# Two group norms share two borders of an attention on one Trainium2 core, and one image's statistics change their place

## The chip, the cores and the metric

The kernel runs on 1 core of one Trainium2 chip, as one program. The metric is the device time of one execution in microseconds (us). It is compared by medians of several runs. The engines of the core that matter here are TensorE (PE: matrix products, with weight loads, PEld, that overlap them), VectorE (DVE), ScalarE (ACT), GpSimd (POOL) and SyncE (SP), which issues most of the DMA transfers.

## The reference

Eight images of 512 channels and 32 x 32 pixels go through two attention blocks. Layer 0 has 8 heads of 64 channels, and its group norm has 32 groups; layer 1 has one head of 512 channels, and its group norm has 8 groups. All numbers are f32.

```python
# layer 0
h = group_norm(x, gn_weight, gn_bias)                  # GROUPS = 32
qkv = jnp.einsum('oc,bct->bot', w_qkv, h.reshape(B, C, T)) + b_qkv[None, :, None]
weight = softmax(jnp.einsum('bct,bcs->bts', q * scale, k * scale))
a = jnp.einsum('bts,bcs->bct', weight, v)
x = x + (jnp.einsum('oc,bct->bot', w_proj, a) + b_proj[None, :, None])
# layer 1
xn = group_norm(x, gamma, beta)                        # GROUPS = 8
q, k, v = conv1x1(xn, ...)
attn = softmax(jnp.einsum('bqc,bck->bqk', q, k) * scale)
x = x + conv1x1(jnp.einsum('bqk,bkc->bqc', attn, v), p_w, p_b)
```

A group norm takes the mean and the variance over the channels of a group and all pixels, and then scales and shifts each channel.

## The kernel before, in words

**Tiling.** An image is four tiles of 128 channels x 1024 pixels. The 1x1 convolutions are Strassen-like products of seven terms, nested twice (`conv2`, `inner_steps`), so that VectorE and GpSimd add blocks while TensorE multiplies. The results of TensorE lie in PSUM tiles; a tile of 128 partitions x 512 f32, which is what `acc_tile` gives out, fills one bank. `acc_tile` has two buffers.

**Order of work.** The main loop of `main_path` runs over the images b. Each pass runs `attention0` of image b, then layer 1 of image b - 1 (`layer1_scores`, `layer1_rest`), then the value, key and query convolutions of image b + 1 (`values`, `keys_and_queries`), then the projection of image b (`projection2`). The first pass has no layer 1, and the last one is laid out otherwise. Every product on TensorE goes through the helper `matmul` at L60, which keeps it in the order of the program text; so a product that waits holds back all later ones. On the other engines a planner places instructions by their traced order and its own forecast of when they are ready, unless one is pinned by `keep_in_program_order`.

**Hooks.** Small work is handed to the large stages as lists of functions. A `conv2` takes four lists, one for each outer pair of its products, called after the pair's seventh step. `attention0` takes the list `extra`: for each of its eight rounds (four pairs of heads by two halves of the pixels) one entry after the round's scores `sc` and one after its products `av`. In a round TensorE makes eight blocks of scores (tiles of 64 rows x 128 columns of the array), ScalarE turns each into `e` (L696), VectorE adds them up in `sum` (L698, L700), and TensorE then multiplies `e` by the values into `av` (tiles of 128 x 64). Entries 4 and 5 are the two borders of the third round: between its scores and its products, and between its products and the next round's scores.

**The norms.** `GroupNorm` computes a norm in four steps. `stats` runs two `bn_stats` and one `bn_aggr` for a channel tile on VectorE (L91, L96). `group_mean` (L107 on) multiplies the means by the matrix of groups on TensorE, copies the product out of PSUM (L113) and makes `dv` of it in three further VectorE instructions (L115, L117, L119). `affine` (L121 on) multiplies `dv` by the same matrix, adds the epsilon on VectorE (`ve`, L124) and makes the scale and the shift in four GpSimd instructions (L126 to L132). `apply` uses them on ScalarE. With `halves` a product is made as two products of 64 columns, the form that the `av` products have; without it as one of 128 columns. Each f32 product appears as two matmul instructions in the trace.

Layer 1's norm of image b, made in `projection2`, puts its two products into entries 4 and 5 of `attention0` of image b + 1. Layer 0's norm of image b + 2 is made in `values` during the pass of image b; its statistics run in the background of the value convolution (in the first pass they are pinned in the value convolution's last two hooks), and its two products stand in the first and third hook of the key convolution, in `keys_and_queries`. There are six such norms of layer 0, for images 2 to 7; the pass of image 6 has none. The norm of image 0 and that of image 1 are made in the prologue. What `affine` yields for image b + 2 is first used in `layer1_rest` of the next pass, where the image is loaded again and normed.

## Time and profile before

| what | value |
|---|---|
| time, median of 3 runs (lowest to highest) | 2768.54 us (2767.63 to 2768.78) |
| time of the profiled execution | 2768.3 us |
| its span, from the first instruction to the last | 2765.8 us |
| granted clock of TensorE, mean | 0.999 |
| products of `gmean` and of `gvar` on TensorE, instructions each | 46 (28 of 128 x 64, 18 of 128 x 128) |
| `rstd` on GpSimd (L126), mean of 16 | 1177 ns |
| `d` (L115) on VectorE, median | 164 ns |
| VectorE busy in the key convolution of the first pass (258.7 to 280.3 us) | 16.56 of 21.60 us |
| VectorE busy in the value convolution of the first pass (233.5 to 258.7 us) | 18.68 of 25.20 us |

How to read it: the span runs from the program's first recorded instruction to its last, and the time of the same execution is 2.5 us longer. Busy time of an engine is the union of its instructions. A row of the timeline gives the start and the length in us, the engine, the line, the operation, what it writes and reads, the shape, how many instructions are merged, and in brackets how long the engine was idle before and what ended that.

### The profile page before, as it was taken

What the parts mean: (1) busy time and instruction counts of PE and PEld (TensorE: products, weight loads), DVE (VectorE), ACT (ScalarE), POOL (GpSimd) and SP (SyncE); (2) the same over time, 40 slices, a digit from 0 to 9 for tenths busy, and PEclk for the clock granted to TensorE, in tenths of its full rate; (3) what the DMA queues carried; (4) which work ended last, traced back from release to release, by engine and by line L of the source; (5) the groups of instructions that cost most, each with busy time, mean ns of one, the idle gap of its engine ahead of it and who ended that gap; (6) DMA issues with size and microseconds to landing.
All of it is one profiled execution on the core that took longest, in us unless ns stands there. A gap on an engine that the chain in (4) does not pass through costs nothing.

```text
span 2765.8 us, 36809 instructions
## 1 busy us (share of the span) xinstructions
PE 2753.6 (100%) x13436; PEld 1762.1 (64%) x13436; DVE 2045.6 (74%) x3214; ACT 998.4 (36%) x1307; POOL 1291.4 (47%) x1384
## 2 busy tenths in 40 slices
PE   9999999999999999999999999999999999999999
PEld 5437736776376853868538694486844968348585
DVE  6587777777777777777777867777678776787776
ACT  1253454214632146312453125531255313633130
POOL 2313605745067440774307752176621766146763
PEclk9999999999999999999999999999999999999999
DMA  7827412344113441144401443114521145112302
GB/s 265 253 91 252 181 32 70 138 159 166 40 63 138 170 162 32 63 161 167 150 24 63 177 182 119 32 55 184 196 98 49 58 153 216 59 54 97 142 24 74
DMA packets 126070, 332.60 MB, mean 120 GB/s; under 512 B 19831, under 2 KB 64695, under 8 KB 114362
## 3 DMA queue, kind: packets, MB, share of 16 engines
q1 hardware_dynamic: 125294, 329.75, 33.6%
q8 instruction: 108, 1.77, 0.3%
q14 instruction: 80, 0.66, 0.1%
q10 hardware_dynamic: 588, 0.42, 0.1%
HBM read 258.14 MB, written 71.99 MB: 119 GB/s over the span
## 4 chain that ended last, share of the span: by engine, by line
PE 99%; DVE 1%; DMA 0%; issue 0%; SPq 0%; DVEq 0%
PE sc L60 16%; PE av L60 16%; PE psb_av L60 6%; PE psb L60 5%; PE psa_av L60 4%; PE psc_av L60 4%; PE psc L60 4%; PE psa L60 3%; PE psb_v L60 3%; PE psb_k L60 3%; PE psb_p L60 3%; PE psb_q L60 3%; PE psb_g L60 3%; PE psb_z L60 3%; PE psc_z L60 2%; PE psa_k L60 2%
## 5 line engine op out<-in xcount | busy, mean ns | idle before, releaser
L700 DVE TENSOR_TENSOR sum<-sum,e 128x1024 f32<-128x1024 f32 x384 | 473.9, 1234 | 35.5 <-ACT e L696 0.9
L696 ACT ACTIVATE e<-sc 128x1024 f32<-128x1024 f32 x512 | 476.1, 1053 | 63.1 <-PE sc L60 62.6
L60 PE MATMUL sc<-q,k 64*128 64x512 f32 x2048 | 456.8, 596 | 0.0
L60 PE MATMUL av<-e,v 128*64 128x512 f32 x2048 | 453.4, 595 | 0.0
L60 PEld LDWEIGHTS sc<-q,k 64*128 64x128 f32 x2048 | 190.1, 185 | 245.9 <-ACT e L696 120.9
L60 PEld LDWEIGHTS av<-e,v 128*64 128x64 f32 x2048 | 141.4, 137 | 299.0 <-issue 288.2
L434 POOL TENSOR_TENSOR inner_h<-x 128x256 f32<-128x256 f32 x16 | 14.8, 924 | 415.9 <-DVE x L1028 415.9
L698 DVE TENSOR_TENSOR sum<-e,e 128x1024 f32<-128x1024 f32 x64 | 79.9, 1249 | 103.6 <-ACT e L696 103.6
L719 ACT COPY a<-av 128x512 f32<-128x512 f32 x64 | 37.5, 586 | 320.1 <-PE av L60 280.6
L126 POOL TENSOR_TENSOR rstd<-ve,mhalf 128x4 f32<-128x4 f32 x16 | 18.8, 1177 | 274.0 <-DVE ve L124 274.0
L60 PE MATMUL psb<-inner,inner_h 128*128 128x256 f32 x448 | 115.6, 380 | 0.0
L60 PE MATMUL psa_av<-e,z 128*128 128x512 f32 x256 | 112.5, 592 | 0.0
L482 ACT COPY psb_v<-psa_v 128x512 f32<-128x512 f32 (+1 forms) x28 | 14.5, 517 | 232.5 <-DVE x L845 176.6
L60 PEld LDWEIGHTS psb<-inner,inner_h 128*128 128x128 f32 x448 | 84.5, 190 | 13.6 <-POOL inner L449 2.1
L60 PE MATMUL psb_z<-w_z,inner_h 128*128 128x128 f32 x672 | 87.5, 276 | 0.0
L60 PE MATMUL psb_g<-inner_h,w_m 128*128 128x256 f32 x336 | 84.9, 381 | 0.0
L776 ACT ACTIVATE e<-e 128x1024 f32<-128x1024 f32 x64 | 65.1, 1052 | 46.7 <-DVE e L766 25.6
L60 PEld LDWEIGHTS psb_z<-w_z,inner_h 128*128 128x128 f32 x672 | 81.4, 192 | 0.5
L60 PEld LDWEIGHTS psa_av<-e,z 128*128 128x128 f32 x256 | 47.4, 190 | 53.6 <-issue 51.7
L771 POOL TENSOR_TENSOR e<-e,e 128x512 f32<-128x512 f32 x64 | 79.3, 1271 | 2.0 <-DVE e L766 1.8
L571 POOL TENSOR_TENSOR v<-v,v 128x256 f32<-128x256 f32 x28 | 20.1, 726 | 125.3 <-DVE u_v L566 121.3
L820 POOL TENSOR_TENSOR t<-e,t 128x1024 f32<-128x1024 f32 x32 | 78.4, 2482 | 0.0
(443 smaller groups left out, 6138.0 us busy)
## 6 DMA issues: line engine op xcount, KB each, us to landing
r<-all_rows SPq DMA_DIRECT2D x78, 256.0 KB
x<-in_x SPq DMA_DIRECT2D x36, 512.0 KB
h<-in_x SPq DMA_DIRECT2D x32, 512.0 KB
spill<-x SPq DMA_DIRECT2D x32, 512.0 KB
x<-spill SPq DMA_DIRECT2D x32, 512.0 KB
out<-x SPq DMA_DIRECT2D x63, 256.0 KB
kept<-a SPq DMA_DIRECT2D x28, 512.0 KB
again<-kept SPq DMA_DIRECT2D x28, 512.0 KB
```

What stands on the lines that cost most here:

```text
L60: tc.keep_in_program_order(nc.tensor.matmul(*args, **kw))
L126: nc.gpsimd.tensor_tensor(rstd, ve, mhalf, ALU.pow)
L434: pin(engine.tensor_tensor(dst, x, y, ALU.subtract))
L482: nc.scalar.copy(ps["b"], ps["a"])
L571: nc.gpsimd.tensor_tensor(d, x, y, ALU.add)
L696: nc.scalar.activation(e, sc, AF.Exp, scale=(C // 8) ** -0.5)
L698: nc.vector.tensor_add(total, es[0], e)
L700: nc.vector.tensor_add(total, total, e)
L719: nc.scalar.copy(dst, av)
L771: nc.gpsimd.tensor_tensor(blocks(dst, r, cc)[0], blocks(x, r, cc)[0], blocks(y, r, cc)[0], ALU.add)
L776: nc.scalar.activation(e[c, cc, r], e[c, cc, r], AF.Exp, scale=scale)
L820: on = lambda *a: lambda: tc.keep_in_program_order(nc.gpsimd.tensor_tensor(*a))
```

## The change

Layer 0's norm of image b + 2 gets `halves=True` and is handed, as `ahead`, to `projection2`. Its two products leave the key convolution for entries 4 and 5 of the next pass's attention. There each entry allocates one PSUM tile and calls the two norms one after the other: layer 1's norm on columns 0 to 3, then layer 0's on columns 4 to 7, with `start=False`. In the first pass the third image's statistics leave the value convolution's hooks 2 and 3 and stand, one channel tile at a time and still pinned, in the four hooks of the key convolution.

```diff
-        def over_group(self, ps, rhs):
+        def over_group(self, ps, rhs, start=True):
             for cols in (ts(0, 64), ts(1, 64)) if self.halves else (slice(0, P),):
-                matmul(ps[cols, :], gm[:, self.layer, cols], rhs, start=True, stop=True)
+                matmul(ps[cols, :], gm[:, self.layer, cols], rhs, start=start, stop=True, skip_group_check=True)
-        def group_mean(self, ps):
+        def group_mean(self, ps, start=True):
...
-            self.over_group(ps, mean)
+            self.over_group(ps, mean, start)
-        def affine(self, ps):
-            self.over_group(ps, self.dv)
+        def affine(self, ps, start=True):
+            self.over_group(ps, self.dv, start)
...
-        def projection2(b, inner, hooks):
+        def projection2(b, inner, hooks, ahead):
...
-            _, _, (mean,), (affine,) = norm_hooks(norm, f"1_{b}")
+            norms = [norm, *([ahead] if ahead else [])]
+            def means():
+                ps = acc_tile(f"gmean_1_{b}")
+                for i, n in enumerate(norms):
+                    n.group_mean(ps[:, ts(i, KC)], i == 0)
+            def affines():
+                ps = acc_tile(f"gvar_1_{b}")
+                for i, n in enumerate(norms):
+                    n.affine(ps[:, ts(i, KC)], i == 0)
             return xt, {
-                0: [lambda c=c: residual(c) for c in range(KC)], 1: stats[:2], 3: [*stats[2:], store], 4: [mean],
-                5: [affine], 7: applies[:2], 9: applies[2:],
+                0: [lambda c=c: residual(c) for c in range(KC)], 1: stats[:2], 3: [*stats[2:], store], 4: [means],
+                5: [affines], 7: applies[:2], 9: applies[2:],
             }
...
-                norm = GroupNorm(0, f"0_{b + 1}", pinned=b == 1)
+                norm = GroupNorm(0, f"0_{b + 1}", pinned=b == 1, halves=True)
                 if b == 1:
...
-                    for i in range(2):
-                        hooks[i + 2] = [*hooks[i + 2], *(lambda c=c: norm.stats(c, xs[c]) for c in (2 * i, 2 * i + 1))]
+                    later_stats = [lambda c=c: norm.stats(c, xs[c]) for c in range(KC)]
...
-        def keys_and_queries(b, f, norm, loads, factors, q_hooks):
-            mean, affine = [], []
-            if norm:
-                mean.append(lambda: norm.group_mean(acc_tile(f"gmean_0_{b + 1}")[:, :KC]))
-                affine.append(lambda: norm.affine(acc_tile(f"gvar_0_{b + 1}")[:, :KC]))
-            k = conv2("k", f, None, f"k0_{b}", [[all_background, *mean], loads, affine, factors])
+        def keys_and_queries(b, f, stats, loads, factors, q_hooks):
+            k = conv2(
+                "k", f, None, f"k0_{b}", [[all_background, *stats[:1]], [*loads, *stats[1:2]], stats[2:3], [*factors, *stats[3:]]]
+            )
...
-            x1, plan = projection2(b, inner_a, p_hooks)
+            x1, plan = projection2(b, inner_a, p_hooks, norm0)
```

More of the change, by code (lines that the diff above doesn't have):

```diff
@@ L1113, in values @@
         def values(b, f, hooks=()):
-            norm = None
+            norm, later_stats = None, []
             if b + 1 < B:
-                norm = GroupNorm(0, f"0_{b + 1}", pinned=b == 1)
+                norm = GroupNorm(0, f"0_{b + 1}", pinned=b == 1, halves=True)
                 if b == 1:
@@ L1127, in values @@
             v = conv2("v", f, None, f"v0_{b}", hooks, by_tokens=True)
-            return lambda s, head: v[head // 2][:, s * P + head % 2 * 64 : s * P + head % 2 * 64 + 64], norm
-        def keys_and_queries(b, f, norm, loads, factors, q_hooks):
-            mean, affine = [], []
-            if norm:
-                mean.append(lambda: norm.group_mean(acc_tile(f"gmean_0_{b + 1}")[:, :KC]))
-                affine.append(lambda: norm.affine(acc_tile(f"gvar_0_{b + 1}")[:, :KC]))
-            k = conv2("k", f, None, f"k0_{b}", [[all_background, *mean], loads, affine, factors])
+            return lambda s, head: v[head // 2][:, s * P + head % 2 * 64 : s * P + head % 2 * 64 + 64], norm, later_stats
+        def keys_and_queries(b, f, stats, loads, factors, q_hooks):
+            k = conv2(
+                "k", f, None, f"k0_{b}", [[all_background, *stats[:1]], [*loads, *stats[1:2]], stats[2:3], [*factors, *stats[3:]]]
+            )
             q = conv2("q", f, pcols("bq0"), f"q0_{b}", q_hooks)
@@ L1235, in main_path @@
                 layer1_rest(b - 1, inner, gf, gsteps, [], [[]] * 4, ahead)
-                v, norm0 = values(b + 1, made["inner"])
+                v, norm0, stats0 = values(b + 1, made["inner"])
                 inner = made["inner"]
             else:
-                v, norm0 = values(1, inner, [[], [], [], [lambda: [f() for f in scaled]]])
+                v, norm0, stats0 = values(1, inner, [[], [], [], [lambda: [f() for f in scaled]]])
             again = [None] * KC
@@ L1261, in main_path @@
             q, k = keys_and_queries(
-                b + 1, inner, norm0, [lambda c=c: load_a(c) for c in range(KC)], [factors_of_a], q_hooks
+                b + 1, inner, stats0, [lambda c=c: load_a(c) for c in range(KC)], [factors_of_a], q_hooks
             )
-            x1, plan = projection2(b, inner_a, p_hooks)
+            x1, plan = projection2(b, inner_a, p_hooks, norm0)
         hf, steps = image_factors(h, f"h1_{B - 1}")
```

## The prediction

> **What bounds the kernel.** I read the page first, then the timeline of TensorE around the products that move, then VectorE beside them, then the few waits of TensorE, then the clock.

> ```profile
> span 2765.8 us, 36809 instructions
> PE 2753.6 (100%) x13436; PEld 1762.1 (64%) x13436; DVE 2045.6 (74%) x3214; ACT 998.4 (36%) x1307; POOL 1291.4 (47%) x1384
> PE 99%; DVE 1%; DMA 0%; issue 0%; SPq 0%; DVEq 0%
> ```

> TensorE is busy all the time and makes up 99% of the chain that ended last. So a product saved is time saved, and a wait of TensorE, which runs in program order, is time lost in full: nothing later has slack to give back. The sum is made against the profiled execution (span 2765.8 us, time 2768.3 us, 0.2 us under the median 2768.54 us of the three runs). A difference within 0.2% (5.5 us) counts as no change.

> **Removed: two products in each of six key convolutions.** Timeline of TensorE, the key convolution of the second pass (with the products) and of the pass of image 6 (without):

> ```profile
> 596.46 1.03 PE L60 MATMUL psb_k<-inner_h,w_k 128*128 128x256 f32 x4
> ...
> 599.91 0.28 PE L60 MATMUL gmean<-mv,gm 128*128 128x4 f32 x2
> 600.05 0.68 PE L60 MATMUL psa_k<-h,w_k 128*128 128x256 f32 x2
> ...
> 618.06 0.81 PE L60 MATMUL psb_q<-inner_h,w_q 128*128 128x256 f32 x3
> ...
> 2285.10 1.03 PE L60 MATMUL psb_k<-inner_h,w_k 128*128 128x256 f32 x4
> ...
> 2306.25 0.81 PE L60 MATMUL psb_q<-inner_h,w_q 128*128 128x256 f32 x3
> ```

> From the first key product to the first query product it is 618.06 - 596.46 = 21.60 us with, and 2306.25 - 2285.10 = 21.15 us without: 0.45 us for the two. Six times that is **-2.7 us**. The five VectorE instructions of the norm (about 0.16 us each) and the four of GpSimd (about 1.6 us) go along. In the attention they cost nothing of themselves: GpSimd was idle 34 us before `rstd` there, and VectorE was idle before `ve`; without this cover they would be 0.8 and 1.6 us on other queues, not on TensorE's. No DMA is moved.

> **Added: the same two products at the two borders.** This is the part that decides. One border pair of the second attention, TensorE and then VectorE:

> ```profile
> 695.83 0.28 PE L60 MATMUL gmean<-mv,gm 128*64 128x4 f32 x4
> 695.97 7.07 PE L60 MATMUL av<-e,v 128*64 128x512 f32 x32
> 702.87 0.23 PE L60 MATMUL gvar<-dv,gm 128*64 128x4 f32 x4
> 703.03 1.56 PE L60 MATMUL sc<-q,k 64*128 64x512 f32 x6
> ...
> 694.63 5.21 DVE L700 TENSOR_TENSOR sum<-sum,e 128x1024 f32<-128x1024 f32 x4
> 699.76 0.15 DVE L113 COPY gmean<-gmean 128x4 f32<-128x4 f32 x1
> ...
> 700.42 1.22 DVE L700 TENSOR_TENSOR sum<-sum,e 128x1024 f32<-128x1024 f32 x1
> ...
> 703.15 0.16 DVE L124 TENSOR_SCALAR ve<-gvar 128x4 f32<-128x4 f32 x1 [0.37 <-PE gvar L60]
> ```

> The products themselves are small: `gmean` delays `av` by 0.14 us and `gvar` delays `sc` by 0.16 us. What counts is the copy at L113. VectorE lags behind TensorE at the end of a round's scores: three more additions of 1.3 us come before the copy, so it starts 3.93 us after its product. Until now nobody on TensorE waited for it before `gvar`, 7 us later. With the change, layer 0's product is traced right after that copy, into other columns of the same bank. Does it wait for the copy? The trace has two cases of one engine in one half of a bank and another engine in the other half:

> ```profile
> 254.22 0.41 DVE L566 TENSOR_TENSOR u_v<-psb_v,v 128x256 f32<-128x256 f32 x1
> ...
> 254.66 0.38 DVE L566 TENSOR_TENSOR u_v<-psb_v,v 128x256 f32<-128x256 f32 x1
> ...
> 255.08 0.49 PE L60 MATMUL psb_v<-w_v,inner_h 128*128 128x128 f32 x2 [0.45 <-DVE u_v L566]
> ...
> 2755.15 4.05 PE L60 MATMUL psc_av<-e,sz 128*128 128x512 f32 x17
> ...
> 2759.24 0.43 DVE L860 TENSOR_TENSOR psc_av<-psc_av,r 128x256 f32<-128x256 f32 x1 [2.03 <-PE psc_av L60]
> ```

> In the first, two additions read the two halves of a bank one after the other; the next product writes the first half, which was free at 254.63, yet it starts only at 255.08, 0.04 us after the second addition's end. In the second, the last product is cut into two halves of eight 256-column instructions (0.216 us apart, so the first half is done near 2757.3); the multiplication of the first half starts at 2759.24, when the second is done, after 2.03 us idle. So this program orders a bank as one thing. I take the wait as real.

> [...]

> **Its price at entry 4.** The copy ends at 699.76 + 0.155 = 699.92; TensorE follows 0.05 us later (the 0.04 above, rounded up), at 699.97; `av` then starts 0.14 us on, at 700.10 or 700.11 in place of 695.97: 4.14 us. Queued behind the waiting product are the 32 products of `av`, and behind those ScalarE's copy of `av` and the next round's exponentials. Nothing takes the stall up: ScalarE only waits for TensorE at that point. In all seven attentions of the trace the copy has the same lag within 0.01 us, and six carry a second norm: 6 x 4.14 = **+24.8 us**. Bounds: nothing (the columns are tracked apart), and 4.14 plus one more addition of 1.3 us ahead of the copy, 5.4 us each.

> **At entry 5.** VectorE is free there. `ve` starts 0.28 us after `gvar` and takes 0.16, and with 0.05 for TensorE the second product starts 0.50 us late; `sc` follows in the same 0.16. 6 x 0.50 = **+3.0 us**, bounds 0 and 4 (one VectorE addition in front in half of the cases).

> **The clock.** A wait of 4.1 us leaves TensorE idle, and this trace has an idle TensorE only at its ends:

> ```profile
> 3.83 3.58 PE L63 MATMUL tr_wk<-ident,rawk 128*128 128x128 f32 x16 [3.83 <-DMA rawk<-in_w]
> ...
> 2759.40:2761.40 2.00, 0.00 (x0) 0.00 (x0) 1.58 (x5) 0.00 (x0) 0.00 (x0) 1.00 0.18 62
> 2761.50:2765.70 4.20, 0.00 (x0) 0.00 (x0) 0.00 (x0) 0.00 (x0) 0.00 (x0) 0.50 0.17 49
> ```

> The second-to-last column but one is the granted clock. It falls to half between 2761.4 and 2761.5, some 2.1 us after TensorE's last product (2759.3). At the start the sixteen products take 0.22 us each against 0.11 to 0.13 for that shape later, so about 3 us of work runs at half rate before full speed is granted. If each 4.1 us wait halves the clock and 3 us of `av` then run at half rate, each loses 1.5 us: 6 x 1.5 = **+9.0 us**. Bounds: 0 (no drop) and 3 us each, 18 us, if it takes twice as long to come back.

> [...]

> **The statistics of the third image.** In the first pass's value convolution two `bn_stats` and a `bn_aggr` (1.2 and 0.2 us for a channel tile) stand before the second `u_v` above, and TensorE's 0.45 us there go with them, with about 0.2 us of weight load that they exposed: -0.6 us. In the key convolution VectorE has 16.56 of 21.60 us busy; one channel tile there is already counted, the norm's own 0.8 us leave, and four tiles of 1.4 us come, so about 19.9. It has idle stretches of 1.27, 0.53 and 1.09 us early on but 0.3 us near the last hook, where the fourth tile and the factors of `a` meet. Bounds 0 and 1.0 us; I take 0.2, since each lump is single and the PSUM tiles there are doubled. Together **-0.4 us**.

> **Sum:** -2.7 + 24.8 + 3.0 + 9.0 - 0.4 = +33.7 us; 2768.3 + 33.7 = **2802 us**.

> **The rivals.** *The wait is real, but the clock stays up.* For it: the only drop is at the end, and two small products of a few columns run just before. Against it: the idle time is twice what preceded that drop. 2768.3 + 24.7 = 2793 us.

> *The copy overtakes the additions.* VectorE's order is a planner's, and a second norm changes its forecast; if the copy came right after the addition that runs at 695.97 to 697.2, two of 1.33 us fewer stand before it, the wait is 1.5 us and the clock holds: 6 x (1.5 + 0.5) - 3.1 = +8.9, 2777 us. Against it: all that is traced before the copy is unchanged, and those additions are traced ahead of it.

> *No wait: the columns of the shared tile are tracked apart.* Then layer 0's products just follow layer 1's. A round with both of a norm's products takes 14.27 us from scores to scores (688.76 to 703.03), one without 14.08 (659.59 to 673.68, the previous rounds): 0.18 us a norm, 1.1 us for six. -2.7 - 0.4 + 1.1 = -2.0: 2766 us, not slower. It decides wherever no copy is waited for; the two half-bank rows speak against it.

> **How the numbers follow.** Forecast 0.60; clock stays up 0.20; copy overtakes 0.09; no wait 0.11. The number is the forecast's, 2802. The range leaves out the last two: down to the clock rival less some 4 us, 2788; up to half of the clock's upper bound more, 2811. Slower by over 0.2% holds the first three cases, 0.88, as the third lies at +0.3%; within 0.2% is the last, 0.10; faster by over 0.2% (below 2763) needs twice the gain of the last, 0.02.

> **What would show it.** At each entry 4 of the first six attentions after the first, four `gmean` instructions, then TensorE idle about 4 us until VectorE's copy, then four more, and `av` after them; no such gap in the last attention. At entry 5 a gap near 0.5 us. The key convolutions take 21.15 us in every pass. The clock shows stretches of half rate of about 3 us after each gap. Eight `gmean` instructions in a row without a gap would make the prediction wrong; so would a copy that follows its product at once.

## The result, and the profile after

The changed kernel takes 2808.46 us (median of 4 runs, 2807.35 to 2810.14) against 2768.66 us; the ratio is 1.0145, 95% interval 1.0131 to 1.016. It is slower by 39.8 us, where 33.7 us were forecast (2802, range 2788 to 2811). The waits are where the prediction put them; the clock cost more than forecast, and one sentence of the argument turned out to be wrong.

The page of the changed kernel, profiled in an execution of 2807.43 us (span; the engines' busy times; the chain that ended last):

```profile
span 2805.5 us, 36858 instructions
PE 2767.2 (99%) x13460; PEld 1765.8 (63%) x13460; DVE 2044.5 (73%) x3214; ACT 998.4 (36%) x1307; POOL 1298.7 (46%) x1384
PE 96%; DVE 3%; DMA 0%; issue 0%; ACT 0%; DVEq 0%; SPq 0%; ACTq 0%
```

VectorE, absent before but for 1%, is now 3% of the chain: TensorE waits for it. The view of TensorE's waits (who waited for whom: total us, times, the longest):

```profile
PE gmean L60 <- DVE gmean L113: 24.6, 6, 4.9
...
PE gvar L60 <- DVE ve L124: 1.6, 6, 0.3
PE psc_v L60 <- DVE x L845: 0.6, 1, 0.6
```

Six waits at entry 4 and six at entry 5, and one that nobody had on the list. The border pair of the second attention, TensorE's timeline:

```profile
700.65 0.28 PE L60 MATMUL gmean<-mv,gm 128*64 128x4 f32 x4
705.14 0.28 PE L60 MATMUL gmean<-mv,gm 128*64 128x4 f32 x4 [4.20 <-DVE gmean L113]
705.28 8.76 PE L60 MATMUL av<-e,v 128*64 128x512 f32 x32
713.87 0.23 PE L60 MATMUL gvar<-dv,gm 128*64 128x4 f32 x4
714.37 0.29 PE L60 MATMUL gvar<-dv,gm 128*64 128x4 f32 x4 [0.26 <-DVE ve L124]
```

and VectorE's:

```profile
703.79 1.22 DVE L700 TENSOR_TENSOR sum<-sum,e 128x1024 f32<-128x1024 f32 x1 [0.46 <-DVE sum L700]
704.93 0.15 DVE L113 COPY gmean<-gmean 128x4 f32<-128x4 f32 x1
...
705.47 0.16 DVE L113 COPY gmean<-gmean 128x4 f32<-128x4 f32 x1 [0.19 <-PE gmean L60]
...
714.15 0.16 DVE L124 TENSOR_SCALAR ve<-gvar 128x4 f32<-128x4 f32 x1 [5.70 <-PE gvar L60]
```

Layer 1's four instructions of `gmean` run at 700.65; layer 0's start at 705.14, right after VectorE's copy, which comes behind the last of its late additions. The same 32 instructions of `av` that took 7.07 us before take 8.76 us here. The windows view says why (length; busy time and instructions of the five engines; granted clock; DMA share; GB/s), here around this border and in the next attention:

```profile
702.40:705.70 3.30, 0.56 (x6) 0.31 (x8) 2.62 (x7) 0.00 (x0) 0.00 (x0) 1.00 0.23 57
705.80:709.10 3.30, 3.30 (x10) 0.90 (x8) 2.62 (x6) 0.00 (x0) 0.00 (x0) 0.50 0.00 0
709.20:712.00 2.80, 2.80 (x16) 0.96 (x14) 0.00 (x0) 0.00 (x0) 0.00 (x0) 1.00 0.46 187
...
1047.10:1053.80 6.70, 5.00 (x16) 1.69 (x18) 4.64 (x12) 0.00 (x0) 0.00 (x0) 0.50 0.13 48
```

In the 3.3 us at half the clock 10 instructions run, in the 2.8 us after it 16. The key convolutions of the later passes have lost their products' 0.45 us (first key product to first query product, 622.88 - 601.73 = 21.15 us):

```profile
601.73 1.03 PE L60 MATMUL psb_k<-inner_h,w_k 128*128 128x256 f32 x4
...
622.88 0.81 PE L60 MATMUL psb_q<-inner_h,w_q 128*128 128x256 f32 x3
```

### The profile page after: what moved, and what is told of

Same layout as the page of the kernel before. It is cut to its first block, busy times and chain, and to the rows that moved or that the text cites. A ratio compares the mean times of both kernels' runs of the same rounds, so it can differ in the third digit from the quotient of the medians.

```text
span 2805.5 us, 36858 instructions
## 1 busy us (share of the span) xinstructions
PE 2767.2 (99%) x13460; PEld 1765.8 (63%) x13460; DVE 2044.5 (73%) x3214; ACT 998.4 (36%) x1307; POOL 1298.7 (46%) x1384
## 4 chain that ended last, share of the span: by engine, by line
PE 96%; DVE 3%; DMA 0%; issue 0%; ACT 0%; DVEq 0%; SPq 0%; ACTq 0%
PE av L60 16%; PE sc L60 15%; PE psb_av L60 5%; PE psb L60 5%; PE psa_av L60 4%; PE psc_av L60 4%; PE psc L60 3%; PE psa L60 3%; PE psb_v L60 3%; PE psb_k L60 3%; PE psb_q L60 3%; PE psb_p L60 3%; PE psb_g L60 3%; PE psb_z L60 3%; PE psc_v L60 2%; PE psc_z L60 2%
## 5 line engine op out<-in xcount | busy, mean ns | idle before, releaser
L700 DVE TENSOR_TENSOR sum<-sum,e 128x1024 f32<-128x1024 f32 x384 | 474.2, 1235 | 36.2 <-DVE sum L700 1.8
L60 PE MATMUL av<-e,v 128*64 128x512 f32 x2048 | 465.2, 608 | 0.0
L60 PE MATMUL sc<-q,k 64*128 64x512 f32 x2048 | 456.8, 596 | 0.0
L60 PEld LDWEIGHTS sc<-q,k 64*128 64x128 f32 x2048 | 190.0, 185 | 246.0 <-ACT e L696 121.2
L60 PEld LDWEIGHTS av<-e,v 128*64 128x64 f32 x2048 | 144.2, 140 | 308.1 <-issue 297.8
L60 PE MATMUL psb<-inner,inner_h 128*128 128x256 f32 x448 | 115.6, 380 | 0.0
L60 PE MATMUL psa_av<-e,z 128*128 128x512 f32 x256 | 112.5, 592 | 0.0
L60 PEld LDWEIGHTS psb<-inner,inner_h 128*128 128x128 f32 x448 | 84.5, 190 | 13.6 <-POOL inner L449 2.1
L60 PE MATMUL psb_z<-w_z,inner_h 128*128 128x128 f32 x672 | 87.5, 276 | 0.0
L60 PE MATMUL psb_g<-inner_h,w_m 128*128 128x256 f32 x336 | 84.9, 381 | 0.0
L60 PEld LDWEIGHTS psb_z<-w_z,inner_h 128*128 128x128 f32 x672 | 81.4, 192 | 0.5
L60 PEld LDWEIGHTS psa_av<-e,z 128*128 128x128 f32 x256 | 47.4, 190 | 53.6 <-issue 51.6
```

The source lines that it names most:

```text
L60: tc.keep_in_program_order(nc.tensor.matmul(*args, **kw))
L700: nc.vector.tensor_add(total, total, e)
```

## The experiments

The theory was that of the prediction: TensorE waits at both borders for VectorE to leave the shared PSUM tile, because of a bank that is ordered as one thing, and the clock falls in the longer wait. Rivals: the extra products or VectorE's extra work cost the time; the order in which copy and product stand in the program makes the wait; the clock costs nothing; the wait goes with the tile and not with the bank.

**1. Both products first** (the same at entry 5 with `affine`; `product=False` leaves out the product inside):

```diff
-                for i, n in enumerate(norms):
-                    n.group_mean(ps[:, ts(i, KC)], i == 0)
+                for i, n in enumerate(norms):
+                    n.over_group(ps[:, ts(i, KC)], n.mv[:, :, 0], i == 0)
+                for i, n in enumerate(norms):
+                    n.group_mean(ps[:, ts(i, KC)], product=False)
```

> Both norms' products are issued one after the other into the same shared tile, and only then come VectorE's copies (at entry 4) and `ve` (at entry 5). Theory (TensorE waits at each border for VectorE to leave the shared bank, and the clock falls in the wait): no wait, no half clock; -2.7 us for the key convolutions, -0.7 us for the third image's statistics, +1.1 us for six pairs of small products: 2766 us. Rival (the extra products at the borders, or VectorE's extra work there, cost the time): stays near 2808 us.

Measured: 2766.53 us against 2768.05 us, ratio 0.9995 (0.9986 to 1.0004). TensorE's timeline at the same border:

```profile
694.39 0.40 PE L60 MATMUL gmean<-mv,gm 128*64 128x4 f32 x8
694.65 7.07 PE L60 MATMUL av<-e,v 128*64 128x512 f32 x32
701.55 0.35 PE L60 MATMUL gvar<-dv,gm 128*64 128x4 f32 x8
701.83 1.56 PE L60 MATMUL sc<-q,k 64*128 64x512 f32 x6
```

Eight instructions in a row, no gap, `av` back at 7.07 us. The added products and VectorE's added work are all there, and the 40 us are gone: that rival falls.

**2. The same with the statistics left in the value convolution**, to price the change's second part:

```diff
-                    later_stats = [lambda c=c: norm.stats(c, xs[c]) for c in range(KC)]
+                    for i in range(2):
+                        hooks[i + 2] = [*hooks[i + 2], *(lambda c=c: norm.stats(c, xs[c]) for c in (2 * i, 2 * i + 1))]
```

> As e1_products_first, but the third image's statistics stay in the value convolution's last two hooks as before. Theory: TensorE's wait of 0.45 us for u_v in the first pass's value convolution comes back, with the weight load behind it: 0.7 us above e1_products_first. Rival (their place makes no difference, or the key convolution pays for them): equal to e1_products_first or below it.

Measured: 2767.78 us, 0.9999 (0.999 to 1.0008), 1.25 us above experiment 1. The intervals overlap, so the times alone don't settle a difference of this size. In the view of TensorE's waits the old one is back, beside one in layer 1 that no other trace has; experiment 1 has neither:

```profile
PE psb_av L60 <- DVE u_av L242: 1.1, 1, 1.1
...
PE psb_v L60 <- DVE u_v L568: 0.5, 1, 0.5
```

The traces give the price. The value convolution of the first pass takes 25.20 us here and 24.48 us in experiment 1, the key convolution behind it 21.15 and 21.24 us: 0.63 us for the two, near the 0.7 expected.

**3. The change's order, but layer 0's products in other banks**, in tiles of their own (the same at entry 5 with `affine`):

```diff
                 for i, n in enumerate(norms):
-                    n.group_mean(ps[:, ts(i, KC)], i == 0)
+                    if i:
+                        ps = ps_pools[0].tile([P, 2, HT], F32, tag="sc", name=f"gmean_0_{b}")[:, 0, :]
+                    n.group_mean(ps[:, :KC])
```

> The order of the program is that of the change (layer 0's product is traced after layer 1's copy), but layer 0's two products go into tiles of their own, in banks of the score tiles that are free at that point. Theory (the shared bank makes the wait): no wait, 2766 to 2767 us. Rival (the order in which copy and product are traced makes the wait): the 4 us gaps stay, near 2808 us.

Measured: 2766.87 us, 0.9996 (0.9986 to 1.0005). TensorE's timeline at the border:

```profile
695.64 0.40 PE L60 MATMUL gmean<-mv,gm 128*64 128x4 f32 x8
695.89 7.07 PE L60 MATMUL av<-e,v 128*64 128x512 f32 x32
702.79 0.35 PE L60 MATMUL gvar<-dv,gm 128*64 128x4 f32 x8
703.07 1.13 PE L60 MATMUL sc<-q,k 64*128 64x512 f32 x4
```

No gap, with the copy still ahead of the product in the program. So sharing makes the wait, not the order alone. But two things were changed at once, the bank and the tile; experiment 9 parts them.

**4. The wait kept, TensorE kept busy in it.**

```diff
+                    if i:
+                        junk = ps_pools[0].tile([P, 2, HT], F32, tag="sc", name=f"junk_{b}")[:, 0, :]
+                        for k in range(4):
+                            for cols in (ts(0, 64), ts(1, 64)):
+                                matmul(junk[cols, :], gm[:, 1, cols], xt[k][:, :HT], start=True, stop=True)
                     n.group_mean(ps[:, ts(i, KC)], i == 0)
```

> The change with its waits, but with eight 512-column products of no use (about 3.4 us, into a free score tile) between layer 1's and layer 0's product at entry 4, so that TensorE works through most of the wait. Theory (the wait takes 25 to 28 us in all, the half clock after it the other 12 to 15): the clock stays up, 2792 to 2796 us. Rival (the clock costs nothing, the wait takes all 40 us): 2808 us.

Measured: 2795.06 us, 1.0097 (1.0082 to 1.0113). TensorE's timeline at the first border:

```profile
357.46 0.28 PE L60 MATMUL gmean<-mv,gm 128*64 128x4 f32 x4
357.60 3.63 PE L60 MATMUL junk<-x,gm 128*64 128x512 f32 x16
361.60 0.28 PE L60 MATMUL gmean<-mv,gm 128*64 128x4 f32 x4 [0.37 <-DVE gmean L113]
361.73 1.49 PE L60 MATMUL av<-e,v 128*64 128x512 f32 x6
```

Layer 0's product still starts 4.14 us after layer 1's, but in the trace's record of the clock it stays full from 9.2 us to the end of the work, here behind the first border (windows view):

```profile
361.60:369.00 7.40, 7.26 (x40) 2.59 (x40) 3.38 (x10) 0.15 (x1) 0.00 (x0) 1.00 0.17 71
```

The kernel is 13.4 us faster than the change for eight products more at each border, and the rival that gave the wait all 40 us falls. The price of the clock is about a microsecond less than these 13.4: the change's trace has a wait of `psc_v` that costs 0.9 us and that this one has not.

**5 and 6. The wait shortened**, by putting layer 0's product of the means behind the second or the third of the eight blocks of `av` (the diff is that of experiment 5; experiment 6 has `s == 2`):

```diff
-                for i, n in enumerate(norms):
-                    n.group_mean(ps[:, ts(i, KC)], i == 0)
+                norms[0].group_mean(ps[:, :KC])
+                if len(norms) > 1:
+                    midway.append(lambda: norms[1].group_mean(ps[:, ts(1, KC)], False))
...
+                        if s == 1 and midway:
+                            midway.pop()()
```

> Layer 0's product of the means stands behind the second of the eight blocks of `av`, so that 1.72 us of the wait are worked through and about 2.4 us are left; entry 5 as in the change. Theory: 6 x (2.4 + 0.5) - 3.4 = +14 us from the waits, 2783 us, and up to 9 us more where the clock still falls: 2783 to 2792 us. Rival (the clock falls only after a whole window of 3.4 us without work): 2783 us, no half clock in the trace.

> As e5_after_block1, behind the third block: 1.6 us of the wait are left. Theory: 6 x (1.6 + 0.5) - 3.4 = +9 us, 2777 us, with the clock up, as less than half of a window of 3.4 us is idle. Rival (any wait of more than a microsecond drops the clock): 2783 us or more.

Measured: 2789.09 us, 1.0078 (1.0061 to 1.0094), and 2779.77 us, 1.0042 (1.0028 to 1.0056). Windows of experiment 5 around two borders with the same wait of 2.1 us, at 1381.5 and at 1041.2, then experiment 6 around a wait of 1.2 us, at 1038.6:

```profile
1382.00:1383.90 1.90, 0.33 (x6) 0.31 (x8) 1.73 (x5) 0.00 (x0) 0.00 (x0) 1.00 0.03 6
1384.10:1387.30 3.20, 3.20 (x10) 0.96 (x8) 2.84 (x7) 0.00 (x0) 0.00 (x0) 0.50 0.00 0
1387.50:1390.00 2.50, 2.50 (x14) 0.86 (x12) 0.00 (x0) 0.00 (x0) 0.00 (x0) 1.00 0.53 213
```

```profile
1042.00:1045.00 3.00, 1.67 (x12) 0.75 (x14) 2.90 (x7) 0.00 (x0) 0.00 (x0) 1.00 0.03 6
1045.00:1049.00 4.00, 3.88 (x22) 1.29 (x18) 1.77 (x6) 0.14 (x1) 0.00 (x0) 1.00 0.32 131
```

```profile
1039.00:1042.00 3.00, 2.19 (x14) 0.89 (x16) 2.79 (x10) 0.00 (x0) 0.00 (x0) 1.00 0.02 5
1042.00:1046.00 4.00, 3.73 (x26) 1.61 (x24) 1.60 (x4) 0.59 (x1) 1.13 (x2) 1.00 0.32 131
```

The same wait drops the clock at one border and not at another; in all, three of experiment 5's six do, and none of experiment 6's. So the clock falls neither only after 3.4 us without work nor after any microsecond of it; the last section says what the drops have in common. Experiment 6 is 2.8 us over its expected 2777, outside it by more than its runs spread. Only 0.5 us of that lies in the waits: its six attentions are 13.1 us longer than those of experiment 1, which has no waits, where 6 x (1.6 + 0.5) = 12.6 were expected. (At one border the wait is 2.8 us; VectorE, which had waited 1.55 us for a transfer in that round, is late there.) Most of the rest is the 3.4 us that the expectation takes off for the moved work: experiment 1, with the same work moved, lies only 1.5 us under the kernel before.

**7 and 8. One border mended, the other left as changed** (the diff of experiment 1 at entry 4 alone, or at entry 5 alone):

> Products first at entry 4 only; at entry 5 layer 0's product still comes after layer 1's `ve`. Theory: 0.5 us at each of six borders stays and nothing else: 3.0 us above e1_products_first, 2769.5 us, clock up. Rival (the wait at entry 5 is hidden by ScalarE's and VectorE's lag behind TensorE): equal to e1_products_first.

> Products first at entry 5 only; the wait at entry 4 and the half clock stay. Theory: 3.0 us under the change's 2808.5 us, 2805.5 us. Rival (the waits are not additive): equal to the change.

Measured: 2770.14 us, 1.0009 (0.9999 to 1.0019), which is 2.2 us above the kernel before where experiment 1 is 1.5 us under it: 3.7 us for the waits at entry 5, 3.0 expected. In its trace layer 0's `gvar` starts 0.50 us behind layer 1's at five borders and 1.19 us at the sixth. And 2807.40 us, 1.0141 (1.0124 to 1.0158): only 1.1 us under the change, 3.0 expected, and only 0.4 us if each is taken against the runs of the kernel before beside it. The waits did shrink as expected, 0.50 to 0.09 us from `gvar` to `gvar`, 2.5 us for six. In its profiled execution, however, the clock was at half for 41.0 us, against 30.7 us in the change's. The other runs on record agree. At a mean granted clock of 0.993 experiment 8 took 2806.12 and 2806.77 us and the change 2809.49; at 0.992 it took 2808.04 and 2808.24 and the change 2810.14; the change's two fastest runs have 0.994, which none of experiment 8's reaches. So at the same clock the gain of 2 to 3 us is there, and a lower clock takes it back. These are four runs of each, from two sessions, and no experiment set the clock apart.

**9. One tile, two banks.** The tile is shared as in the change, but it is a score tile of 2 x 512 columns, and each norm has a half of it (the same at entry 5):

```diff
-                ps = acc_tile(f"gmean_1_{b}")
+                ps = ps_pools[0].tile([P, 2, HT], F32, tag="sc", name=f"gmean_1_{b}")
                 for i, n in enumerate(norms):
-                    n.group_mean(ps[:, ts(i, KC)], i == 0)
+                    n.group_mean(ps[:, i, :KC])
```

> The order of the change and one tile shared by both norms at each border, but a score tile of two banks: layer 1's columns lie in its first bank, layer 0's in its second. Theory as the runs stand (the bank is what is waited for): no wait, 2766 to 2767 us. Rival (the wait is for the tile, whatever its banks): the 4 us gaps and the half clock stay, near 2808 us.

Measured: 2807.72 us, 1.0144 (1.0128 to 1.0159): the rival's number. TensorE's timeline:

```profile
700.53 0.28 PE L60 MATMUL gmean<-mv,gm 128*64 128x4 f32 x4
705.02 0.28 PE L60 MATMUL gmean<-mv,gm 128*64 128x4 f32 x4 [4.21 <-DVE gmean L113]
705.16 1.50 PE L60 MATMUL av<-e,v 128*64 128x512 f32 x4
```

The two norms lie in different halves of the tile, and the gap is the change's, 4.21 us of idle time against 4.20. Together with experiment 3 (two tiles, no gap) it shows that sharing the tile is enough for the wait, also where the norms have a half each. That a half is a bank is the author's account of the layout; no run shows it. Two tiles in one bank were not run. The theory falls in this one point.

**10. Experiment 1's kernel again**, for its gain:

> The same kernel as e1_products_first, for a narrower interval against the kernel before. Theory: 2.0 us under it (2.7 + 0.7 - 1.4), 0.9993; e1_products_first gave 1.5 us. Rival (the two gains are given back at the borders or by VectorE in the key convolution): 1.000.

Measured: 2766.80 us against 2768.14 us, 0.9996 (0.9987 to 1.0005). Twice 1.3 to 1.5 us under the kernel before, each time with an interval that reaches over 1: likely the best of the kernels here, but not by more than the measurement can tell.

## Why the prediction was right, and where it was not

The profiled executions differ by 2805.5 - 2765.8 = 39.7 us. By the prediction's steps:

| step | forecast | measured in the trace | how it is read |
|---|---|---|---|
| products out of the key convolutions | -2.7 | -2.7 | 21.60 to 21.15 us, six times (experiment 2 has 21.15 in the first pass too) |
| waits at entry 4 | +24.8 | +26.3 | from layer 1's to layer 0's `gmean`: 4.14 four times, 4.49, 5.23 |
| waits at entry 5 | +3.0 | +3.0 | from `gvar` to `gvar`, 0.50 six times |
| half clock | +9.0 | +12.8 | six attentions are 42.05 us longer, less the two rows above; 0.7 of it is not the clock's (below) |
| the third image's statistics | -0.4 | -0.6 | first pass, value and key convolution 46.80 to 45.72 us, less the first row's 0.45 |
| a wait not foreseen | | +0.9 | one value convolution, `psc_v` for `x`, 20.07 in place of 19.20 us |

The misses lie nearly all on one side and add up to 6.0 us; no errors cancelled. The time fell inside the range because the range had left room above for a dearer clock.

**The waits** were right, in place, mechanism and price: layer 0's product behind VectorE's copy, the copy behind three late additions, 4.14 us. Experiments 1, 3 and 4 show that the wait is there and costs what was said: experiment 4 lies 28.5 us above experiment 1, where 24.8 + 3.0 = 27.8 were forecast for the waits. The two longer ones are VectorE's own lateness, which a bound of one addition more had allowed for. In the sixth, VectorE's queue waits in the same round for a transfer (its timeline):

```profile
2076.99 0.25 DVE L662 RECIPROCAL recs<-cols 128x16 f32<-128x16 f32 x1 [1.09 <-DMA cols<-rows]
```

The lag of the second, 0.35 us, goes with the 0.46 us of idle time before an addition in VectorE's timeline above; it is there in experiment 1 too, and what it is stays open.

**The reason given for the wait was wrong in one word.** The prediction read from two rows "this program orders a bank as one thing". In both rows the two halves were also halves of one tile, so the rows couldn't tell bank and tile apart, and experiment 9 decides for the tile. The number was not touched by it, since in the change the two norms share a tile as well. By banks, experiment 9 was expected to have no wait, and it has the same one: 24.5 us in six waits for the copy, 24.6 in the change.

**The clock term was mis-sized:** 9.0 us forecast, about 12 us in the trace. The step took 3 us of work at half rate after each wait, from the start of the program, 18 us in all. In the trace three of the six stretches at half clock last 3.41 us and three 6.83 us, 30.7 us together. TensorE is idle in 6.0 us of them, as the longer ones begin inside the wait; the other 24.7 us of work at half rate lost half of their length, 12.3 us (as `av` above lost 8.76 - 7.07 = 1.69 us in 3.41). The 12.8 of the table holds 0.7 us more: in experiment 4, at full clock, the six attentions are also that much longer than their waits explain (0.06 us each, 0.37 in the fifth). That every wait halves the clock was the author's estimate. In the trace all six did, and in only one of them was TensorE idle through all of the 3.41 us before the drop; in the others it was idle for 2.13 to 2.81 us of them.

**The statistics** gained what their wait had cost, and of the 0.2 us set aside for the key convolution 0.09 are seen, the first pass's 21.24 us against 21.15. The wait of `psc_v` for `x` is in the value convolution of the third pass, where none of the moved work stands. Experiment 9 has it as well, 3 and 6 have half of it, and the others do not. Where it appears, VectorE's timeline has a wait for the transfer of the image whose statistics run there, and behind it VectorE is busy without a break until `x`:

```profile
1261.93 0.69 DVE L91 BATCH_NORM_STATS2 bnst<-ahead 128x6 f32<-128x512 f32 x1 [0.84 <-DMA ahead<-in_x]
```

The traces without the wait have no such line in that pass. Why the transfer landed later in some executions stays open.

**The rivals.** "No wait" was the right account of what the change would be without its sharing: 2766 us, and experiments 1, 3 and 10 give 2766.5 to 2766.9. "The clock stays up" is experiment 4: 2793 forecast, 2795.06 measured.

## What to carry to other kernels

Before two results share a PSUM tile, ask in which order they are traced: in this program a product that is traced after another engine's read of the same tile waits for that read, though its columns, and even its half of the tile, are others (4.20 us of idle time in the change, 4.21 in experiment 9). Issue all products into a shared tile first and read afterwards, or give each its own tile. And price such a wait by the reader's lag at that point, not by the length of the read: the copy takes 0.15 us, and TensorE waited 4.1 us for it because VectorE was three additions behind.

## What the runs showed of the hardware

**How much of a step was idle.** I laid the grid over TensorE's idle times in the change's trace (the ends of its instructions are modelled, so the last digit is rough). The six drops between work:

| half clock from (us) | idle in the step before, at full clock (us) | idle in the first step at half clock (us) | idle in the second (us) |
|---|---|---|---|
| 361.00 | 3.41 | 0.33 | |
| 705.75 | 2.81 | 0.00 | |
| 1047.08 | 2.13 | 1.72 | 0.00 |
| 1395.24 | 2.32 | 0.00 | |
| 1736.57 | 2.32 | 1.54 | 0.00 |
| 2081.32 | 2.50 | 2.45 | 0.00 |

The step before the drop at the end of the program was idle for 2.47 us; each other step at full clock was idle for 1.54 us or less, and full clock followed it. A step with 1.54 us without work was followed by full clock where the clock was full (1388.4 to 1391.8) and by half where it was at half (1736.6 to 1740.0); full speed came back after steps with 0.33 us or less. So in this trace the way back took more work than staying up did. The dearest waits are the three that left 2.13 us or more without work in the step before the drop and 1.54 us or more in the next, which is at half clock: one more step at half clock followed. Experiment 8 has one of this kind too (windows view):

```profile
355.70:359.00 3.30, 1.48 (x10) 0.53 (x8) 3.09 (x3) 2.80 (x4) 0.00 (x0) 1.00 0.52 141
359.10:362.40 3.30, 1.37 (x8) 0.75 (x10) 2.87 (x8) 0.00 (x0) 0.00 (x0) 0.50 0.08 18
362.50:365.80 3.30, 3.30 (x10) 0.94 (x8) 1.91 (x5) 0.00 (x0) 0.00 (x0) 0.50 0.14 58
366.00:369.00 3.00, 3.00 (x16) 0.98 (x14) 0.00 (x0) 0.00 (x0) 0.00 (x0) 1.00 0.20 81
```

A wait that straddles two steps can also be the cheapest. Experiment 6's longest, 2.8 us, lies with some 1.2 us in one step and 1.6 us in the next, and the clock stays up (windows view):

```profile
2055.50:2058.70 3.20, 2.08 (x10) 0.43 (x6) 2.99 (x3) 0.78 (x1) 0.00 (x0) 1.00 0.52 147
2058.80:2062.10 3.30, 1.74 (x12) 0.74 (x14) 3.09 (x8) 0.00 (x0) 0.00 (x0) 1.00 0.05 12
```

So a wait of some 2 to 3 us cost no step or one here, and one of 4 us cost one or two: in these traces the price of a wait is not a smooth function of its length.
